# Layer 0 of a four-layer network: x read in 4 KB runs, the group norm's gap filled, pair terms stored by POOL, attention's first rows fed on chip

## The chip, the cores and the metric

The kernel runs on one core of one Trainium2 chip. The metric is the device time of one execution in microseconds (us), as the median of three runs. The engines are PE (matrix products and transposes; PEld is its weight load), DVE (vector), ACT (scalar functions), POOL (general) and SP, which here only issues DMAs. DMAs issued by SP and those issued by POOL run on the same 16 DMA engines of the core. PE writes to PSUM; DVE and ACT read PSUM and SBUF, POOL reads SBUF.

## What is computed

x has 256 x 256 tokens of 128 channels, float32. Four layers follow one another; each takes a group norm of x, computes something from it and adds the result to x. Only layer 0 and the start of layer 1 matter here:

```python
def _L0_conv_ref(x, mask, ln_w, ln_b, w_tri, w_q, w_k, w_v, w_g, b_g, w_o, b_o):
    # H = 4 heads of C = 32; B, I, J, D = 1, 256, 256, 128
    mu = jnp.mean(x, axis=-1, keepdims=True)
    var = jnp.mean(jnp.square(x - mu), axis=-1, keepdims=True)
    xn = (x - mu) * jax.lax.rsqrt(var + EPS) * ln_w + ln_b
    tri_bias = jnp.einsum('bijd,dh->bhij', xn, w_tri)[:, None]
    mask_bias = INF * (mask[:, :, None, None, :] - 1.0)
    q = (xn @ w_q).reshape(B, I, J, H, C) * (1.0 / np.sqrt(C))
    k, v = ...                                   # the same with w_k, w_v
    scores = jnp.einsum('bimhc,binhc->bihmn', q, k) + tri_bias + mask_bias
    attn = jax.nn.softmax(scores, axis=-1)
    o = jnp.einsum('bihmn,binhc->bimhc', attn, v)
    g = jax.nn.sigmoid((xn @ w_g + b_g).reshape(B, I, J, H, C))
    return (g * o).reshape(B, I, J, H * C) @ w_o + b_o

x = x + _L0_conv_ref(_gn(x), ...)    # _gn: mean and variance of 32 groups of 4 channels over all tokens
x = x + _L1_conv_ref(_gn(x), ...)
...
```

The group norm needs all of x before anything else can be computed. The layer norm then needs mean and variance of every token. The tri_bias ("pair term") of one row i of x is needed by every row of attention, so all of x has to be passed over a second time before the first row's softmax.

## The kernel before

`x` lies in memory token by token. The kernel works on its transpose (channels on the 128 partitions), in 32 tiles of SC = 2048 tokens. Tiles 0 to 17 are written transposed to memory (`xT`) in the first pass and read again in the second; tiles 18 to 31 are held in SBUF and written to `xT` during the second pass, because attention reads all of it. CK is 512, P and D are 128, NH is 4, N is 256. Outside of `manual_schedule` the instructions are put into an order by a scheduler; within it, each engine has them in the order of the program.

The first pass, and the folding of weights that follows in the program:

```python
RES = NSC // 2 + 2
with tc.tile_pool(name="x0", bufs=1) as xres, tc.tile_pool(name="p0", bufs=3) as sb:
    held = {s: xres.tile([P, SC], F32, name=f"x0_{s}") for s in range(RES, NSC)}
    with tc.tile_pool(name="p0ps", bufs=6, space=PSUM) as ps:
        for s in range(NSC):
            xt = sb.tile([P, 4, 4, D], F32, name="p0_x", tag="xt")
            nc.sync.dma_start(xt, x_tok[s * SC : (s + 1) * SC, :].rearrange("(c p k) d -> p c k d", p=P, k=4))
            xc = held[s] if s in held else sb.tile([P, SC], F32, name="p0_xc", tag="xs")
            for c in range(4):
                pt = ps.tile([P, P, 4], F32, name="p0_t")
                for k in range(4):
                    nc.tensor.transpose(pt[:, :, k], xt[:, c, k, :], ident)
                pf = pt.rearrange("p n k -> p (n k)")
                nc.vector.bn_stats(stats0[:, s * 4 + c, :], pf)
                nc.scalar.copy(xc[:, c * CK : (c + 1) * CK], pf)
            if s not in held:
                nc.sync.dma_start(xT[:, s * SC : (s + 1) * SC], xc)
    with tc.tile_pool(name="f0", ...) as fsb, tc.tile_pool(name="f0ps", ...) as ps:
        ...   # w0c, cqkg, cv, w2c_, b2w, wsum, kcol, ctri from the weights: small matmuls and copies
```

The second pass: per token the sums that the layer norm needs and the pair terms (`pr`, five rows: four heads and the mean), and the mean of squares (`e2`):

```python
    order = [s for i in range(RES) for s in (RES + i, i) if s < NSC]     # 18, 0, 19, 1, ...
    for _ in range(3):
        fetch(0)                                                          # reads of xT, three ahead
    m0, r0 = gn_finish(stats0, "gn0")                                     # bn_aggr of all entries, then the groups
    ...
    for i, s in enumerate(order):                                         # in manual order
        xc = held[s] if s in held else loaded[s]
        sq = sb.tile([P, SC], F32, name="p1_sq", tag="xt")
        nc.scalar.activation(sq, xc, AF.Square, bias=mrneg, scale=r0)
        pr = ps.tile([P, CK], F32, name="p1_pr")
        ...                                                               # 4 matmuls into pr
        tr = wk_sb.tile([P, CK], F32, name="p1_tr", bufs=3)
        nc.vector.tensor_copy(tr, pr)
        if s in held:
            nc.sync.dma_start(xT[:, s * SC : (s + 1) * SC], xc)
        else:
            fetch(i)
        for c in range(4):
            nc.sync.dma_start(triD[:, s * SC + c * CK : s * SC + (c + 1) * CK], tr[32 * c : 32 * c + 5, :])
        ...                                                               # 4 matmuls of the sq before into e2
    for c in range(4):
        nc.sync.dma_start(mean[32 * c : 32 * c + 32, :], by_c[c])         # the means back, from triD
    ...                                                                   # mean, square, e2 - square, max, Sqrt
    nc.vector.reciprocal(mean, var)
    for c in range(4):
        nc.sync.dma_start(rs_c[c], mean[32 * c : 32 * c + 32, :])         # 1/std to memory (rsD)
```

The setup of attention, up to its loop:

```python
    nc.sync.dma_start(tri..., triD...)                                    # pair terms, a pool of its own ("p2i")
    nc.sync.dma_start(mk, mbD...)
    nc.sync.dma_start(rs, rsD...)                                         # 1/std back from memory
    for h in range(NH):
        ... (tri + toff) * rs                                             # DVE
    ...                                                                   # 20 transposes, + ctri on DVE: triT, mbT
    load(0)        # x of group 0 (4 rows) from xT, 1/std of it from rsD, broadcast to all partitions
    prepare(0)     # ACT: x - mean; POOL: times 1/std
    tiles(0)
    for c in range(2):
        for what in "qkvg":
            project(0, what, c)
    load(1)
    prepare(1)
    for j in range(2 * NG + 5):
        ...        # the loop over pairs of rows
```

Layer 1 begins with a folding of its own. Its tile `cen` lies in a pool ("f1") whose room the first loads of layer 1 take over:

```python
    with tc.tile_pool(name="f1", bufs=1) as sb, tc.tile_pool(name="f1ps", ...) as ps:
        ...                                         # v1, v2, vb1, vb2, wgf, bgf: need the group norm
        nc.tensor.matmul(pb, lhsT=wz0, rhs=ln2b, ...)
        cen = sb.tile([P, 4, 32], F32, name="f1_c")
        ...                                         # memset, 8 affine_select on POOL
        nc.vector.tensor_scalar(wz4, wz4, g4, None, ALU.mult)
        nc.tensor.matmul(pw, lhsT=cen..., rhs=wz4, ...)
        nc.vector.tensor_copy(wzc, pw)
```

Of the kernel before, what the change touches and what calls it, by code (L numbers as in the profile page):

```python
# [8 lines left out]
F32 = mybir.dt.float32  # L9
# [22 lines left out]
def kernel(ctx: ExitStack, tc: tile.TileContext, a: dict, out: bass.AP):  # L32
# [127 lines left out]

    def gn_finish(stats, name):

        mv = const.tile([P, 2], F32, name=name + "_mv")
        nc.vector.bn_aggr(mv, stats.rearrange("p n s -> p (n s)"))
        return gn_groups(mv, name)
# [38 lines left out]
    w0c = const.tile([P, 4 * D + NH], F32, name="w0c")  # L204
    slide = const.tile([P, 63], F32, name="slide")
# [3 lines left out]
    with tc.tile_pool(name="x0", bufs=1) as xres, tc.tile_pool(name="p0", bufs=3) as sb:  # L209
        held = {s: xres.tile([P, SC], F32, name=f"x0_{s}") for s in range(RES, NSC)}  # L210
        with tc.tile_pool(name="p0ps", bufs=6, space=PSUM) as ps:
            for s in range(NSC):
                xt = sb.tile([P, 4, 4, D], F32, name="p0_x", tag="xt")
                nc.sync.dma_start(
                    xt, x_tok[s * SC : (s + 1) * SC, :].rearrange("(c p k) d -> p c k d", p=P, k=4)
                )
                xc = held[s] if s in held else sb.tile([P, SC], F32, name="p0_xc", tag="xs")
                for c in range(4):
                    pt = ps.tile([P, P, 4], F32, name="p0_t")
                    for k in range(4):  # L220
                        nc.tensor.transpose(pt[:, :, k], xt[:, c, k, :], ident)
                    pf = pt.rearrange("p n k -> p (n k)")
                    nc.vector.bn_stats(stats0[:, s * 4 + c, :], pf)
                    nc.scalar.copy(xc[:, c * CK : (c + 1) * CK], pf)
                if s not in held:
                    nc.sync.dma_start(xT[:, s * SC : (s + 1) * SC], xc)

        with tc.tile_pool(name="f0", bufs=1) as fsb, tc.tile_pool(name="f0ps", bufs=1, space=PSUM) as ps:
            cen = fsb.tile([P, P], F32, name="f0_c")
            nc.vector.tensor_scalar(cen, ident, -1.0 / D, None, ALU.add)  # L230
            wa = fsb.tile([P, 4 * D + NH], F32, name="f0_a")
            nc.vector.tensor_scalar(wa, w0, ln_w, None, ALU.mult)
            wb = fsb.tile([P, 4 * D + NH], F32, name="f0_b")
            nc.vector.tensor_scalar(wb, w0, ln_b, None, ALU.mult)
            for lo, hi in ((0, 4 * D), (4 * D, 4 * D + NH)):
                pc = ps.tile([P, hi - lo], F32, name="f0_pc", tag=f"f0_pc{lo}")
                nc.tensor.matmul(pc, lhsT=cen, rhs=wa[:, lo:hi], start=True, stop=True)
                nc.vector.tensor_copy(w0c[:, lo:hi], pc)
# [1415 lines left out]
```

## Time and profile before

| | before |
|---|---|
| median of 3 runs | 3493.64 us (3487.25 to 3499.86) |
| span of the profiled execution | 3506.8 us |
| PE, DVE, ACT, POOL busy | 89%, 66%, 56%, 46% of the span |
| DMA | 759.49 MB, mean 217 GB/s |

The page cuts the span into 40 slices of 87.7 us and gives for each engine the busy share in tenths. PE is at 3, 6, 7, 5 in the first four slices and at 9 from the fifth on to the seventeenth, which is attention. A busy share over the whole span says nothing about any one stage; for that the trace is asked for stretches of time. A line of instructions reads: start, duration, engine, line of the program, operation, output and inputs, and in brackets how long the engine stood idle before it and what released it. A line of waits reads: engine and line that waited, what it waited for, the sum in us, how many times, the longest. "SPq" is SP issuing DMAs; an instruction of the DMA kind is listed at its issue, not at its landing.

### The profile page before, as it was taken

How to read it: one execution, taken by the hardware profiler on the slowest of the kernel's cores; microseconds unless marked ns; L12 is line 12 of the kernel's file. 1: busy time of each engine (PE TensorE's matmuls, PEld its weight loads, DVE VectorE, ACT ScalarE, POOL GpSimd, SP SyncE). 2: the span in 40 equal slices, each digit the busy share in tenths (PEclk: the TensorE clock that was granted, in tenths of full speed). 3: DMA queues.
4: the chain of work that ended last, by engine and by line, in shares of the span. 5: the costliest groups of instructions: out<-in, count | busy, mean ns of one | idle time of the engine just before them, and what ended most of it. 6: DMA issues, size and time to landing. Idle time of an engine off the chain costs nothing.

```text
span 3506.8 us, 52443 instructions
## 1 busy us (share of the span) xinstructions
PE 3133.7 (89%) x20260; PEld 1652.1 (47%) x20260; DVE 2321.5 (66%) x2637; ACT 1961.4 (56%) x2198; POOL 1605.4 (46%) x821
## 2 busy tenths in 40 slices
PE   3675999999999999966597899999999999959998
PEld 3512555555555555521432344444899533314444
DVE  4624888888888888852388454544555677747776
ACT  3563777777777777733243454443444466636655
POOL 4002777777777777732488000000555354514343
PEclk7887999999999999978799899999999999969999
DMA  9883333333333333349599686775999899747664
GB/s 334 324 317 113 98 123 114 106 122 115 105 122 111 109 122 112 108 156 387 173 321 356 228 312 244 284 270 193 342 353 351 307 335 322 277 168 204 193 200 133
DMA packets 309867, 759.49 MB, mean 217 GB/s; under 512 B 77627, under 2 KB 148957, under 8 KB 259437
## 3 DMA queue, kind: packets, MB, share of 16 engines
q1 hardware_dynamic: 298749, 746.43, 60.9%
q0 software_dynamic: 10864, 9.65, 0.9%
q8 instruction: 162, 2.65, 0.3%
q14 instruction: 92, 0.75, 0.1%
HBM read 468.28 MB, written 287.66 MB: 216 GB/s over the span
## 4 chain that ended last, share of the span: by engine, by line
PE 38%; DMA 7%; DVE 2%; ACT 1%; SPq 1%; issue 1%; POOL 0%; ACTq 0%; DVEq 0%; POOLq 0%
PE p_pm L946 13%; PE tp_z L1612 6%; PE p_pm L1099 4%; PE p_pm L1334 4%; PE p_pg L810 3%; DMA x3T<-p_x 2%; PE tp_a L1601 2%; PE p_st L903 1%; PE p_pt L1371 1%; PE p_pz L818 1%; DMA p_er<-eD 1%; DMA x2T<-p_x 1%; DMA p_x<-x3T 1%; PE p_eb L860 1%; PE p_rz L860 1%
## 5 line engine op out<-in xcount | busy, mean ns | idle before, releaser
L489 DVE TENSOR_TENSOR p_e<-p_S,triT 128x1024 f32<-128x1024 f32 x512 | 609.0, 1211 | 144.7 <-PE p_S L479 144.7
L499 POOL TENSOR_TENSOR p_es<-p_e 128x1024 f32<-128x1024 f32 x256 | 603.1, 2367 | 127.4 <-issue 67.3
L497 ACT ACTIVATE p_e<-p_e,mbT 128x1024 f32<-128x1024 f32 x512 | 551.8, 1137 | 63.0 <-DVE p_e L489 61.2
L946 PE MATMUL p_pm<-p_zn,wf 128*128 128x512 f32 x1040 | 450.0, 594 | 1.4 <-DVE p_zn L963 1.4
L464 PE MATMUL p_mm<-p_xn,wf 128*128 128x512 f32 x768 | 409.2, 617 | 9.2 <-POOL p_xn L437 9.2
L437 POOL TENSOR_TENSOR p_xn<-p_xn,p_rs 128x1024 f32<-128x1024 f32 x64 | 153.5, 2398 | 452.2 <-DMA p_rs<-rsD 259.9
L946 PEld LDWEIGHTS p_pm<-p_zn,wf 128*128 128x128 f32 x1040 | 197.6, 191 | 254.6 <-issue 247.8
L479 PE MATMUL p_S<-p_q,p_k 32*128 32x256 f32 x4096 | 295.4, 400 | 5.0 <-DVE p_e L489 5.0
L479 PEld LDWEIGHTS p_S<-p_q,p_k 32*128 32x128 f32 x4096 | 185.8, 184 | 161.5 <-PE p_mm L455 91.7
L1348 POOL TENSOR_TENSOR p_q<-p_q,p_pb 128x2024 f32<-128x2024 f32 x32 | 144.1, 4503 | 254.8 <-DVE p_pb L1342 254.8
L1612 PE MATMUL tp_z<-p_B,tp_at 128*128 128x256 f32 x1024 | 250.2, 387 | 2.4 <-DMA p_B<-bD 2.2
L512 PE MATMUL p_o<-p_e,p_v 128*32 128x256 f32 x4096 | 249.2, 384 | 0.0
L1012 POOL DMA_DIRECT2D rs__18024<-rs2D x4 | 2.1, 520 | 531.7 <-PE p_pm L946 531.7
L1055 POOL TENSOR_TENSOR k<-k,p_sq 128x512 f32<-128x512 f32 x128 | 163.1, 1274 | 135.2 <-ACT p_sq L1053 135.2
L1165 POOL TENSOR_TENSOR p_x<-p_x,p_g 128x2048 f32<-128x2048 f32 x30 | 136.2, 4542 | 171.9 <-DVE p_g L1152 137.8
L1612 PEld LDWEIGHTS tp_z<-p_B,tp_at 128*128 128x128 f32 x1024 | 185.1, 191 | 24.5 <-issue 2.5
L464 PEld LDWEIGHTS p_mm<-p_xn,wf 128*128 128x128 f32 x768 | 126.8, 191 | 114.6 <-issue 90.3
L1054 DVE TENSOR_TENSOR k<-tp_z,k 128x512 f32<-128x512 f32 x128 | 88.6, 692 | 128.4 <-ACT p_sq L1053 128.4
L512 PEld LDWEIGHTS p_o<-p_e,p_v 128*32 128x32 f32 x4096 | 120.4, 110 | 110.1 <-ACT p_g L470 41.5
L979 DVE SCALAR_TENSOR_TENSOR p_b<-p_pm,b2w,p_b 128x1024 f32<-128x1024 f32 x64 | 82.2, 1284 | 126.6 <-PE p_pm L946 112.2
L455 PEld LDWEIGHTS p_mm<-wf,p_xn 128*128 128x128 f32 x1024 | 135.3, 192 | 62.8 <-issue 61.9
L1051 ACT COPY p_K<-tp_z 128x512 f32<-128x512 f32 x128 | 74.9, 585 | 159.7 <-PE tp_z L1612 159.7
(353 smaller groups left out, 5903.8 us busy)
## 6 DMA issues: line engine op xcount, KB each, us to landing
p_x<-x2T SPq DMA_DIRECT2D x64, 1024.0 KB
p_x<-x1T SPq DMA_DIRECT2D x48, 1024.0 KB
p_x<-in_x_dram SPq DMA_DIRECT2D x32, 1024.0 KB
p_x<-xT SPq DMA_DIRECT2D x64, 512.0 KB
p_rs<-rsD SPq DMA_DIRECT2D x64, 512.0 KB
p_rb<-rzD SPq DMA_DIRECT2D x256, 128.0 KB
x1T<-p_x SPq DMA_DIRECT2D x64, 512.0 KB
aD<-p_a SPq DMA_DIRECT2D x32, 1024.0 KB
```

Of the source, the lines that this page charges most:

```text
L437: nc.gpsimd.tensor_tensor(xn, xn, t["rs"], ALU.mult)
L464: nc.tensor.matmul(pm, lhsT=w, rhs=t["xn"][:, cs_], start=True, stop=True)
L479: nc.tensor.matmul(Ss[h // 2][:, h % 2, u, :], lhsT=t["k"][hp, r * N + u * P : r * N + (u + 1) * P], rhs=t["q"][hp, r * N : (r + 1) * N], ...
L489: nc.vector.tensor_tensor(e[:, :, 2 * p : 2 * p + 2, :].rearrange("p u h n -> p h u n"), Ss[p], triT[:, 2 * p : 2 * p + 2, :, :], ALU.add,)
L497: nc.scalar.activation(e[:, u, :, :], e[:, u, :, :], AF.Exp, bias=mbT[:, u, i : i + 1])
L499: nc.gpsimd.tensor_tensor(es, e[:, 0, :, :], e[:, 1, :, :], ALU.add)
L512: nc.tensor.matmul(t["o"][hp, r % 2, :], lhsT=t["v"][:, r * 2 + u, hp], rhs=e[:, u, h, :], start=(u == 0), stop=(u == 1),)
L946: nc.tensor.matmul(pm[:, c, :], lhsT=wf2[:, i, :], rhs=zns[s][:, k * CK : (k + 1) * CK], start=True, stop=True)
L1055: nc.gpsimd.tensor_tensor(k2, k2, sq, ALU.add)
L1099: nc.tensor.matmul(pm[:, c, :], lhsT=w, rhs=src[:, k * CK : (k + 1) * CK], start=True, stop=True)
L1348: nc.gpsimd.tensor_tensor(q[:, :, 1 : N - 2], q[:, :, 1 : N - 2], pb[:, :, 0 : N - 3], ALU.add)
L1612: nc.tensor.matmul(pz[:, t, :], lhsT=at[:, u, t * P : (t + 1) * P], rhs=Bc[:, u, :], start=(u == 0), stop=(u == 1))
```

## The change

It touches only what lies before attention's loop and the beginning of layer 1. What it does, and what for:

- **First pass.** A partition takes 8 tokens in a row (4 KB) instead of 4 (2 KB), so that a load has half as many pieces. The eight transposes of a block lie side by side in a PSUM tile[...]; the interleaving of tokens is done by ACT, which reads that tile with a stride. The pass is in manual order: the load of three tiles ahead is issued right after a tile's transposes, before its store.
- **Folding.** The folding of all weights, layer 1's `bz` and `wzc` included, is done after tile 12 of the first pass.
- **Group norm.** All statistics but the last four entries are aggregated one tile early and merged with the rest afterwards; meanwhile the first five held tiles are stored to `xT`.
- **Second pass.** POOL issues the stores of the pair terms.
- **Setup.** 1/std stays on chip (`rs0`): a matmul with a selector broadcasts it for the first 1024 tokens, and transposes turn it for the pair terms, which are loaded and turned while it is still being computed. Only the first half of group 0 is projected before the loop.

```diff
+            def load0(s):
+                if s < NSC:
+                    xts[s] = sb.tile([P, 2, 8, D], F32, name="p0_x", tag="xt")
+                    nc.sync.dma_start(
+                        xts[s], x_tok[s * SC : (s + 1) * SC, :].rearrange("(c p k) d -> p c k d", p=P, k=8)
+                    )
+            def folds():
+                ...   # the folding of layers 0 to 3, two PSUM buffers
+            for s in range(3):
+                load0(s)
             for s in range(NSC):
...
-                for c in range(4):
-                    pt = ps.tile([P, P, 4], F32, name="p0_t")
-                    for k in range(4):
-                        nc.tensor.transpose(pt[:, :, k], xt[:, c, k, :], ident)
...
+                for c in range(2):
+                    pt = ps.tile([P, 8, P], F32, name="p0_t")
+                    for k in range(8):
+                        nc.tensor.transpose(pt[:, k, :], xt[:, c, k, :], ident)
+                    for h in range(2):
+                        nc.vector.bn_stats(stats0[:, s * 4 + 2 * c + h, :], ...)
+                    nc.scalar.copy(
+                        xc[:, c * 2 * CK : (c + 1) * 2 * CK].rearrange("p (n k) -> p n k", k=8),
+                        pt.rearrange("p k n -> p n k"),
+                    )
+                load0(s + 3)
                 if s not in held:
                     nc.sync.dma_start(xT[:, s * SC : (s + 1) * SC], xc)
+                if s == 12:
+                    folds()
+                if s == NSC - 2:
+                    mv_first = gn_part(stats0, 0, T // CK - 4, "gn0_a")
...
-        m0, r0 = gn_finish(stats0, "gn0")
+        early = range(RES, RES + 5)
+        for s in early:
+            nc.sync.dma_start(xT[:, s * SC : (s + 1) * SC], held[s])
+        mv0 = gn_merge(mv_first, gn_part(stats0, T // CK - 4, T // CK, "gn0_b"), 1.0 - 4.0 * CK / T, "gn0_mv")
+        m0, r0 = gn_groups(mv0, "gn0")
...
-                    if s in held:
+                    if s not in held:
+                        fetch(i)
+                    elif s not in early:
                         nc.sync.dma_start(xT[:, s * SC : (s + 1) * SC], xc)
-                    else:
-                        fetch(i)
                     for c in range(4):
-                        nc.sync.dma_start(
+                        nc.gpsimd.dma_start(
                             triD[:, s * SC + c * CK : s * SC + (c + 1) * CK], tr[32 * c : 32 * c + 5, :]
                         )
...
+                nc.scalar.activation(mean, mean, AF.Square, bias=off[:, 4:5])
...
+                nc.vector.reciprocal(rs0, var)
...
+            load_x(0)
+            tri = ...                                   # load of the pair terms, of the mask, of x for group 1
+            for c in range(4):
+                nc.sync.dma_start(rs_c[c], rs0[32 * c : 32 * c + 32, :])
+            load_rs(1)
+            xn = centre(0)
+            ...                                         # 20 transposes; ACT copies, + toff: triT, mbT
+            rb = [...]                                  # two matmuls: rs0 broadcast for tokens 0 to 1023
+            ...                                         # four transposes: rsT
             tiles(0)
             for c in range(2):
-                for what in "qkvg":
-                    project(0, what, c)
-            load(1)
+                nc.vector.tensor_tensor(xn[:, c * CK : (c + 1) * CK], xn[...], rb[c], ALU.mult)
+                for h in (2 * c, 2 * c + 1):
+                    nc.vector.tensor_tensor(triT[:, h, :, :], triT[:, h, :, :], rsT, ALU.mult)
+            project(0, "q", 0)
+            project(0, "k", 0)
+            for h in range(NH):
+                nc.scalar.activation(triT[:, h, :, :], triT[:, h, :, :], AF.Identity, bias=ctri[:, h : h + 1])
+            project(0, "v", 0)
+            project(0, "g", 0)
             prepare(1)
             for j in range(2 * NG + 5):
...
+                if j == 0:
+                    for what in "qkvg":
+                        project(0, what, 1)
...
-    with tc.tile_pool(name="f1", bufs=1) as sb, tc.tile_pool(name="f1ps", bufs=1, space=PSUM) as ps:
+    with tc.tile_pool(name="f1ps", bufs=1, space=PSUM) as ps:
...                                                      # bz, cen, wz4, wzc gone from here
```

## Prediction

> **What bounds the kernel now.** I read the page's slices first (which engine is full when), then the table of busy time by stretches cut at the borders of the change, then the waits of the DMA-issuing engine SP, and last the timeline around each border. The stretches are: first pass over x, group norm, second pass over x, setup of attention, attention, start of layer 1, its first pass.
>
> ```profile
> 0.00:164.00 164.00, 78.49 (x512) 73.36 (x512) 84.37 (x147) 74.62 (x128) 35.27 (x73) 0.77 0.94 338
> 164.00:182.00 18.00, 14.83 (x74) 8.23 (x78) 10.55 (x31) 8.52 (x8) 0.00 (x0) 0.72 0.37 143
> 182.00:278.00 96.00, 64.80 (x486) 17.07 (x478) 21.23 (x38) 58.98 (x29) 0.00 (x0) 0.86 0.87 323
> 278.00:318.00 40.00, 13.44 (x48) 8.48 (x48) 12.96 (x16) 6.51 (x8) 2.34 (x1) 0.62 0.38 119
> 318.00:1537.00 1219.00, 1206.07 (x12260) 668.38 (x12259) 1020.43 (x1083) 865.14 (x954) 900.47 (x383) 0.99 0.34 110
> 1537.00:1563.00 26.00, 5.98 (x35) 3.84 (x37) 12.91 (x23) 1.54 (x2) 1.40 (x8) 0.57 0.45 165
> ```
>
> The last two figures of a row are the DMA share and GB/s; before them come PE, PEld, DVE, ACT, POOL and the clock. Both passes over x are DMA-bound (0.94 and 0.87). The group norm (18 us) and the setup (40 us) are bound by nothing that is full: they are chains. Attention is bound by PE, 1206 of 1219 us, and the change leaves its loop alone. So all it can earn lies in the 318 us ahead of attention and in the 26 us behind it.
>
> The waits of SP, first pass, then second pass:
>
> ```profile
> SPq L226 <- ACT p_xc L224: 49.0, 18, 6.8
> SPq L214 <- PE p_t L221: 38.6, 15, 3.8
> ```
> ```profile
> SPq L336 <- DMA p_xc<-xT: 25.0, 15, 3.2
> SPq L336 <- DMA xT<-x: 11.5, 13, 1.2
> ```
>
> In the first pass SP stands before stores that wait for copies while free buffers could be loaded. In the second, the small pair stores (L336) wait for large transfers to land: by the order of the issues, SP can go on only when the DMA issued eight before has landed (POOL shows the same count in the weights: its ninth waited 2.11 us for its first), and eight of every ten DMAs here are 10 KB stores. So hardly more than one load and one store are in flight.
>
> The timeline at the borders:
>
> ```profile
> 37.55 0.38 DVE L694 TENSOR_SCALAR wz<-wz,g 128x128 f32<-128x128 f32 x1 [16.39 <-DMA g<-in_L_conv_ln_g_dram]
> ...
> 164.11 3.62 DVE L164 BATCH_NORM_AGGREGATE gn_mv<-stats 128x2 f32<-128x768 f32 x1
> ...
> 175.34 2.10 ACT L321 ACTIVATE p_sq<-x,mrneg,gn_rstd 128x2048 f32<-128x2048 f32 x1 [0.47 <-DVE mrneg L294]
> ...
> 281.32 0.48 DVE L353 TENSOR_SCALAR p_mean<-p_mean,p_off 128x512 f32<-128x512 f32 x1 [4.86 <-DMA p_mean<-triD]
> ...
> 284.58 3.35 DVE L358 RECIPROCAL p_mean<-p_var 128x512 f32<-128x512 f32 x1 [0.79 <-ACT p_var L357]
> ...
> 293.88 2.74 DVE L391 SCALAR_TENSOR_TENSOR tri<-tri,toff,p_rs 128x512 f32<-128x512 f32 x4 [5.96 <-DMA p_rs<-rsD]
> ...
> 307.19 2.34 POOL L437 TENSOR_TENSOR p_xn<-p_xn,p_rs 128x1024 f32<-128x1024 f32 x1 [259.89 <-DMA p_rs<-rsD]
> ...
> 319.57 2.35 DVE L489 TENSOR_TENSOR p_e<-p_S,triT 128x1024 f32<-128x1024 f32 x2 [1.24 <-PE p_S L479]
> ```
> ```profile
> 1557.47 0.29 DVE L697 COPY wzc<-f_w 128x128 f32<-128x128 f32 x1 [0.89 <-PE f_w L696]
> 1557.51 0.33 SPq L707 DMA_DIRECT2D x<-x1T  x1
> ...
> 1562.87 3.29 PE L712 MATMUL p<-x,v 128*32 128x512 f32 x16 [5.44 <-DMA x<-x1T]
> ```
>
> Layer 1's weight folding, pulled ahead by the scheduler, holds DVE 16.4 us in the first pass. Statistics end at 164.1 and the second pass starts 11.2 us later. In the setup 1/std goes to memory and back twice (to 293.88 for the pair terms, to 307.19 for x). At 1557.5 the first load of layer 1 waits until the folding lets go of its buffer.
>
> **What the Trainium skill says.** "Perfetto Trace Analysis", section "DMA Optimizations", holds that 2 KB pieces made into 4 or 8 KB can improve throughput dramatically. The trace does not promise that: 54.37 MB in 91.4% of the first 164 us is 363 GB/s of busy queue with mostly 2 KB pieces; the second pass, mostly 8 KB, moves 30.90 MB in 86.7% of 96 us, 371 GB/s. "DMA: Bandwidth & Descriptors", section "Issuing engines are not separate DMA queues", says that another issuing engine saves only issue time; here it should also give SP its places in flight back. The same page, section "Anatomy of one DMA — SWDGE (gpsimd) path", gives some 2 us fixed per DMA issued by POOL; this trace has 5.2 to 5.4 us to landing for tiny weight loads beside full queues. "ScalarE: Activation LUTs", section "What ACT_TABLE_LOAD costs", gives about 280 ns + 0.833 ns per element: 1.13 us for 1024, and the trace has 1.137 for Exp of that size, 1.016 for a plain copy out of PSUM. It says nothing of a strided read of PSUM, which the new copy does.
>
> **The change part by part.**
>
> *First pass.* 32 loads and 18 stores of 1.049 MB are 52.4 MB. Now they end near 160 and the last statistics at 164.1, 4 us of lag. At 367 GB/s, midway between the two rates because runs of x double, they take 143 us; the weights (2.5% of 164) add 4, the start 2. Laying transposes side by side saves nothing on PE: 273 ns median here, 273 in layer 3's contiguous ones. The folding, now in order after tile 12, costs about 13 us of DVE and PE: 8 us that its matmuls spanned at 164.8, 2 of scalings then done early, 3.2 of the group-mean matrix at 1554.6. Of this the queue (two loads and a store, some 8 us) hides most; 3 to 5 us stay. The 10 us of DMA idle (6% of 164) shrink to little else. Sum: 143 + 4 + 2 + 4 (folding) + 4 (lag) = 157, less some 2 us that runs of 4 KB may save beyond the midway rate: last statistics at **155**, gain **9**.
>
> *Group norm.* Of the 3.62 us aggregation all but four entries lie earlier; five small DVE steps of 0.16 to 0.22 come in. The part from there to the first Square took 2.5 us (172.84 to 175.34). So 4.3 us instead of 11.2. The 7 us do not count by themselves, since the second pass is DMA-bound: what counts is that the queue stays full. Five stores, 5.2 MB or 14 us, behind three prefetches do that.
>
> *Second pass.* From the last landing of x, 155 - 4 = 151: 18 loads and 14 stores, 33.55 MB at 371 GB/s, are 90 us, pair terms and mask (1.8 MB) 5. At a busy share of 0.97 that is 98; plus 3 us from landing to the last pair copy gives 252, where it was 276.5. ACT needs 32 x 2.09 = 67 us, so it isn't the bound. Gain at this point **24**, the first pass included.
>
> *Setup.* Before: last pair copy at 276.5, first bias add 319.6: 43 us. After: four POOL stores 2.2 us (0.53 each in the weights), landing 2.5, mean loads 1.7 + 1.7, then Square to reciprocal 6.4 as now: 1/std at +14.5 (now +11.5, as SP's stores cost less). The raw pair terms arrive and are turned by about +16, beside it. Then broadcast and turning of 1/std on PE 3, first half of x and two pair planes on DVE 2, q and k 3.5 with a cold clock, v and g 3, scores 1: the first add at about +28. That is 15 us less; the second half of group 0's projections (4.1 us by 1.02 each) moves into the first rows, where PE has little room. Net **11**.
>
> *Start of layer 1.* Without the folding's buffer, its first load can go out at about 1548 with the two others. DMA stands idle from about 1554 to 1558 now and the pass after it is DMA-bound (0.95). Gain **5**.
>
> Sum: 24 + 11 + 5 = 40; 3493.6 - 40 = **3453 us**.
>
> **The rivals.**
>
> *POOL's pair stores become the bound of the second pass.* Eight in flight with 5.3 us to landing is 0.66 us per store, 2.65 per tile, against 2.8 of DMA per megabyte at 371 GB/s: nearly equal. With 6.5 us to landing it is 3.25 per tile, 104 us from 160: the second pass ends at 264 and the gain falls to 28 (3466). For it: 51.4 us of DVE waiting for these stores already. Against it: POOL has nothing else to do then.
>
> *The strided copy out of PSUM is slow.* If 1024 elements cost 2.2 us instead of about 1.1, ACT needs 4.4 per tile; the 14 tiles that are only loaded, at 2.8 now, lose 22 us: 3475. No row here shows such a read, for or against.
>
> *The queue fills perfectly.* No stall of the folding, 376 GB/s throughout, POOL free: 148 for the first pass, 243 for the second, and the setup earns 15: gain 54, 3440. For it: shares of 0.98 in the tail of the first pass (120 to 150 us).
>
> *Attention gives it back.* Its start could be pushed by the second half of the projections and the wait for group 1's 1/std through memory; 5 us at most, since both were on the path before.
>
> **Range and chances.** The first two rivals bound it above, the third below; with a few us of spread between runs (3487 to 3500 before) I take 3436 to 3472. A gain of over 2%, 70 us, would need more than all idle DMA time of the two passes and the whole setup; a loss of 70 has no mechanism. Faster 0.03, same 0.95, slower 0.02.
>
> **What would show it.** Last statistics near 155, first Square within 5 us of it with the DMA share over 0.9 through the gap; last pair copy near 252, SP no longer waiting for landings at the pair stores, POOL perhaps doing so; first bias add some 28 us after the last pair copy; the first load of layer 1 issued with its neighbours. Wrong would be: a copy much over 1.2 us per 1024 elements, DVE waiting over 50 us for the pair stores, or a DMA share in the passes no better than before.

## The result, and the profile after

The changed kernel takes 3471.67 us (median of 4 runs, 3464.3 to 3479.48), the kernel before in the same comparison 3491.65. The ratio is 0.994 with a 95% interval of 0.9911 to 0.997: some 20 us gained, where 40 were predicted (3453) and up to 3472 allowed for. Both kernels were compared once more on another occasion, with a ratio of 0.9908 (0.9883 to 0.9934) and medians 28 us apart. Runs of one kernel spread over 15 us and more, so below the stages are compared by the trace and only the sums by the medians.

Stretches of the changed kernel, cut at the same events as before the change (columns: stretch in us, its length, busy us of PE, PEld, DVE, ACT and POOL, granted clock, DMA share, GB/s):

```profile
0.00:162.00 162.00, 97.38 (x550) 83.53 (x550) 92.43 (x175) 64.79 (x64) 36.71 (x81) 0.75 0.89 350
162.00:167.00 5.00, 1.17 (x4) 1.00 (x4) 1.85 (x12) 2.66 (x4) 0.00 (x0) 0.50 1.00 423
167.00:264.00 97.00, 65.80 (x514) 16.22 (x514) 23.66 (x41) 66.52 (x33) 59.91 (x121) 0.92 0.84 315
264.00:295.00 31.00, 11.06 (x58) 7.61 (x58) 8.93 (x10) 8.15 (x13) 3.53 (x8) 0.63 0.33 113
295.00:1516.00 1221.00, 1207.43 (x12262) 668.91 (x12258) 1024.04 (x1088) 868.15 (x959) 900.57 (x383) 0.99 0.33 110
1516.00:1537.00 21.00, 3.02 (x28) 2.58 (x32) 9.22 (x15) 1.54 (x2) 0.00 (x0) 0.50 0.56 201
```

The group norm shrank from a gap of 11 us with a mostly idle queue to 5 us with a full one. Attention is as long as before. But the DMA share, which was to rise, is *lower* in the first pass (0.89, was 0.94) and in the second (0.84, was 0.87). The first pass is cut finer here:

```profile
40.00:68.00 28.00, 17.39 (x93) 15.83 (x94) 13.22 (x21) 10.12 (x10) 8.22 (x15) 0.63 1.02 413
68.00:98.00 30.00, 18.21 (x76) 14.43 (x73) 12.23 (x38) 3.60 (x4) 1.57 (x8) 0.60 0.43 174
98.00:160.00 62.00, 41.55 (x274) 35.43 (x272) 45.59 (x69) 34.88 (x35) 0.00 (x0) 0.83 1.01 398
```

A full queue at about 400 GB/s on both sides (a share of 1 or a little above is a full queue), and a hole of 30 us at less than half of that. In the hole lies the weight folding. The waits of SP, first pass and then second pass, and those of DVE and POOL in the second:

```profile
SPq L240 <- PE p_t L331: 81.0, 24, 24.3
SPq L343 <- ACT p_xc L337: 33.9, 18, 2.5
```
```profile
SPq L357 <- PE p_pr L421: 57.6, 12, 7.1
SPq L403 <- DVE mk L402: 11.8, 1, 11.8
```
```profile
DVE p_tr L427 <- DMA triD<-p_tr: 52.4, 22, 6.0
...
POOL triD L433 <- DMA triD<-p_tr: 22.0, 23, 1.8
```

One load of x (L240) stood 24.3 us before tiles that PE had not transposed. In the second pass SP no longer waits for landings, as predicted. It waits for a buffer of x that PE is still to read; PE waits for DVE; DVE waits 52.4 us for the pair stores of three tiles before; and POOL, which issues them, waits for its own landings. The timeline at the borders:

```profile
74.05 0.23 DVE L255 TENSOR_SCALAR f_s<-ident 128x128 f32<-128x128 f32 x1 [3.83 <-issue]
...
92.85 0.29 DVE L321 COPY wzc<-f_w 128x128 f32<-128x128 f32 x1 [0.95 <-PE f_w L320]
...
96.01 1.01 ACT L337 COPY p_xc<-p_t 128x1024 f32<-128x1024 f32 x1 [24.69 <-PE p_t L331]
...
162.23 0.26 DVE L164 BATCH_NORM_AGGREGATE gn_b<-stats 128x2 f32<-128x24 f32 x1
...
167.28 2.09 ACT L418 ACTIVATE p_sq<-x,mrneg,gn_rstd 128x2048 f32<-128x2048 f32 x1 [0.42 <-DVE mrneg L372]
...
263.28 0.69 DVE L427 COPY p_tr<-p_pr 128x512 f32<-128x512 f32 x1 [1.57 <-DMA triD<-p_tr]
...
273.52 3.35 DVE L453 RECIPROCAL rs<-p_var 128x512 f32<-128x512 f32 x1 [0.79 <-ACT p_var L452]
276.95 0.39 SPq L633 DMA_DIRECT2D tri<-triD  x1
...
295.24 2.36 DVE L550 TENSOR_TENSOR p_e<-p_S,triT 128x1024 f32<-128x1024 f32 x2 [1.45 <-PE p_S L540]
...
1515.79 3.62 DVE L745 BATCH_NORM_AGGREGATE chk_mv<-stats 128x2 f32<-128x768 f32 x1
...
1525.35 3.62 DVE L181 BATCH_NORM_AGGREGATE gn_mv<-stats 128x2 f32<-128x768 f32 x1 [4.70 <-DVEq L754]
...
1531.37 0.17 DVE L200 RECIPROCAL gn_rstd<-gn_sd 128x1 f32<-128x1 f32 x1 [0.99 <-ACT gn_sd L198]
1531.56 0.33 SPq L791 DMA_DIRECT2D x<-x1T  x1
...
1536.60 3.33 PE L796 MATMUL p<-x,v 128*32 128x512 f32 x16 [3.73 <-issue]
```

The lines of before that belong beside these, where the prediction does not show them:

```profile
275.77 0.69 DVE L330 COPY p_tr<-p_pr 128x512 f32<-128x512 f32 x1 [2.64 <-DMA triD<-p_tr]
...
1540.50 3.62 DVE L638 BATCH_NORM_AGGREGATE chk_mv<-stats 128x2 f32<-128x768 f32 x1
...
1547.06 3.62 DVE L164 BATCH_NORM_AGGREGATE gn_mv<-stats 128x2 f32<-128x768 f32 x1 [1.64 <-SPq L647]
```

Against before: last pair copy done at 263.97 (was 276.46, 12.5 earlier); from there to attention's first bias add 31.3 us (was 43.1, 11.8 less); attention to its last aggregation at 1515.79 1220.6 us (was 1220.9); from there to the first matmul of layer 1 20.8 us (was 22.4). Together 26 us. The last of these hides two parts. Between attention's last aggregation and the group norm's (the two lines with chk_mv and gn_mv) lies a branch of the program, behind which DVE stood idle 4.70 us (was 1.64). From the group norm's aggregation to the matmul it took 11.3 us (was 15.8), 4.6 less. Four holes are left to explain: the folding (68 to 98), the second pass that is not full, the load of the pair terms (276.95) that goes out only after the reciprocal, and layer 1's first load (1531.56), which does the same.

### The profile page after: what moved, and what is told of

Its sections match the earlier page's. It is cut to its first block, busy times and chain, and to the rows that moved or that the text cites. A ratio compares the mean times of both kernels' runs of the same rounds, so it can differ in the third digit from the quotient of the medians.

```text
span 3477.7 us, 52488 instructions
## 1 busy us (share of the span) xinstructions
PE 3130.0 (90%) x20268; PEld 1652.2 (48%) x20268; DVE 2319.3 (67%) x2639; ACT 1957.9 (56%) x2144; POOL 1666.4 (48%) x948
## 4 chain that ended last, share of the span: by engine, by line
PE 38%; DMA 11%; DVE 2%; SPq 2%; issue 2%; ACT 1%; POOL 1%; ACTq 0%; DVEq 0%; POOLq 0%
PE p_pm L1030 13%; PE tp_z L1696 7%; PE p_pm L1183 6%; DMA p_x<-x3T 3%; DMA x2T<-p_x 2%; PE p_pm L1418 2%; DMA abD<-p_ab 2%; PE tp_a L1685 2%; PE p_pg L894 2%; PE p_st L987 2%; DMA p_t<-tD 1%; PE p_rz L944 1%; PE p_rk L944 1%; SPq L1305 1%; PE p_pz L902 1%
## 5 line engine op out<-in xcount | busy, mean ns | idle before, releaser
L516 PEld LDWEIGHTS p_mm<-wf,p_xn 128*128 128x128 f32 x1024 | 134.4, 191 | 61.9 <-issue 59.8
## 6 DMA issues: line engine op xcount, KB each, us to landing
p_rb<-rzD SPq DMA_DIRECT2D x256, 128.0 KB
```

## The experiments

Each is an edit of the changed kernel. First that kernel itself, as a control.

> The changed kernel again, nothing edited: 3472 us within 8. Last statistics near 162, first Square near 167, last pair copy near 264, first bias add near 295. It stands here so that the edits of it are read against it on the same chip.

Measured: 3470.82 us (3462.75 to 3482.41); last statistics at 160.71, first Square at 165.77, last pair copy done at 263.26, first bias add at 296.00. What follows is compared with 3471. The runs were made on four occasions, on which the kernel before had medians from 3495 to 3512 us. So a few us between medians of different occasions show little by themselves, and the stages are read from the traces.

**The folding in pieces.** The folding becomes a generator with 14 `yield` lines, two of them in loops of two, so it runs in 17 pieces; after every half tile from tile 9 on one piece is issued. Its scratch gets a pool of its own, as it now lives longer.

```diff
-                scratch = sb.tile([P, SC], F32, name="f0_s", tag="xs")
+                scratch = fsb.tile([P, SC], F32, name="f0_s")
...
+                yield                      # after each step of folds() that the next one waits for
...
+                    if s >= 9:
+                        next(fold, None)
                 load0(s + 3)
...
-                if s == 12:
-                    folds()
```

> The folding of the weights is cut into 15 pieces, one after each half tile from tile 9 on, with scratch room of its own; nothing else differs from the changed kernel. Theory: done in one piece after tile 12 it stopped PE and DVE for some 19 us and emptied the DMA queue (share 0.43 from 68 to 98 us), so cut up the last statistics come at 147 instead of 162 and the time falls by 15 us, to 3457. Rival: the folding costs its own work wherever it stands, because DVE and PE have little room in the first pass: no more than 5 us.

Measured: 3452.26 us (3448.52 to 3455.08), 18.6 less than the control. The same stretch in its trace, and the last statistics:

```profile
68.00:98.00 30.00, 20.98 (x128) 18.80 (x126) 17.57 (x38) 12.15 (x12) 1.57 (x8) 0.77 1.02 424
```
```profile
143.37 0.26 DVE L164 BATCH_NORM_AGGREGATE gn_b<-stats 128x2 f32<-128x24 f32 x1
```

The queue is full throughout (1.02 for 0.43), the last statistics come at 143.37 instead of 160.71, and the 17 us reach the end. The folding is a chain in which DVE and PE wait for each other: 18.8 us from 74.05 to 92.85 in the changed kernel. Engines in strict order did nothing for x meanwhile. SP issued nothing between 71.35 and 96.04, and what was in flight kept the queue full only to about 80 us; from 82 to 95 it moved 4 GB/s. In pieces the same chain has other work between its steps. One thing is not kept apart: before the chain DVE stood 3.83 us. The scratch takes one of the three buffers of the stores in the changed kernel, and this edit also gives it room of its own. Whether that was the wait, and so up to 3.8 of the 18.6 us, is not shown.

**The mask ahead.** The mask's load, its conversion and its store to memory move from the start of the second pass to tiles 4 and 6 of the first.

```diff
-            mk = wk_sb.tile([P, 2, N], F32, name="mk", bufs=1)
-            nc.sync.dma_start(mk, a["L0_conv_mask"]...)      # and its conversion, and the store to mbD
...
+                if s == 4:
+                    mk = msb.tile([P, 2, N], F32, name="mk")
+                    nc.sync.dma_start(mk, a["L0_conv_mask"]...)
+                if s == 6:
+                    ...                                      # conversion, store to mbD
```

> The mask is loaded, converted and stored during tiles 4 to 6 of the first pass instead of at the start of the second; nothing else differs from the changed kernel. Theory: in the second pass the mask's load lies behind eight megabytes that now fill the gap, SP stands 11.8 us before the mask's store and cannot issue reads of x, and the DMA share falls to 0.36 between 176 and 184 us; with the mask gone from there the share stays over 0.9 and the time falls by 8 us, to 3464. Rival: POOL's pair stores bound the second pass at about 3 us per tile anyway, so it falls by 2 us at most.

Measured: 3475.31 us (3466.32 to 3485.54), no gain. SP's wait at the mask is gone, yet from first Square to last pair copy it takes 102.1 us where the control takes 97.5. DVE waits for the pair stores for 61.9 us (52.4 in the changed kernel):

```profile
DVE p_tr L428 <- DMA triD<-p_tr: 61.9, 20, 8.4
```

The mask was not what ended this pass. That the pair stores were is shown by the run with half as many stores below.

**Pair stores by SP again.** One word: the stores of `p1_tr` are issued by `nc.sync` instead of `nc.gpsimd`.

> The pair stores are issued by SP again; nothing else differs from the changed kernel. Theory that POOL's stores (5.5 us to landing, eight in flight) bound the second pass: it gets shorter by about 5 us, DVE's 52 us of waiting for these stores falls below 25, and the mean is back sooner after the last pair copy. Rival, the purpose of the change: SP's places in flight are what matters, and the second pass gets longer by 5 to 10 us, with SP waiting for landings of x at the pair stores (25 us in the kernel before).

Measured: 3472.94 us, ratio to before 0.9932 (0.9911 to 0.9954) against the control's 0.9908 (0.9883 to 0.9934). Six of its 20 executions, and eight of the 20 of the run on layer 1's first load below, lie apart at 3510 to 3524 us, and without them the medians are 3471.4 and 3473.1. Neither expectation shows in the time, and this part of the change is not seen to earn anything: in the changed kernel SP's waits for landings went, and the same kind of wait came up at POOL. That agrees with the Trainium skill, "DMA: Bandwidth & Descriptors", section "Issuing engines are not separate DMA queues", by which another issuing engine saves only the time of issuing, and not with the places in flight that I added to it.

**Runs of 2 KB again.**

```diff
-                    xts[s] = sb.tile([P, 2, 8, D], F32, name="p0_x", tag="xt")
+                    xts[s] = sb.tile([P, 4, 4, D], F32, name="p0_x", tag="xt")
...              # the load with k=4, and the transposes and the copy that fit it
```

> The changed kernel with one thing put back: x is loaded in runs of 2 KB again (each partition takes four consecutive tokens in each of four blocks, not eight in each of two); transposes side by side, the one copy of 1024 per half tile and all else stay. Theory (longer runs move more per busy us): outside the folding's window the first pass falls from 387-394 GB/s to about 360 at the same DMA share near 1, so its 52 MB take some 9 to 11 us longer and the whole kernel 8 to 11 us: about 3481. Rival (the gain came from loads issued ahead of the stores, and the run length is indifferent): DMA rate within 5 GB/s of the changed kernel's, time within 3 us of 3471. A rate that falls while the time stays would say that something else ends the first pass.

Measured: 3475.59 us (3472.68 to 3478.46), 4 to 5 more, on another occasion than the control.

```profile
40.00:68.00 28.00, 15.72 (x90) 14.42 (x89) 13.14 (x21) 10.10 (x11) 9.03 (x16) 0.76 1.04 408
98.00:160.00 62.00, 38.47 (x267) 33.53 (x265) 43.39 (x66) 33.84 (x34) 0.00 (x0) 0.86 1.02 377
```

The first of these stretches before the change:

```profile
40.00:68.00 28.00, 13.34 (x86) 12.89 (x84) 15.18 (x27) 13.32 (x24) 6.45 (x11) 0.70 0.89 308
```

408 for 413, 377 for 398. Seven traces with the unchanged first pass have between 373 and 398 in the second stretch, 387 in the mean, so the run length is worth some 10 GB/s there if anything, under 2 us of the 62. The last statistics come at 162.93, inside what those traces spread over (159.1 to 164.9). The large gain that the Trainium skill, "Perfetto Trace Analysis", section "DMA Optimizations", holds possible is not there, and the rise from 308 GB/s between 40 and 68 us (before) to 413 has another cause.

**The store ahead of the load.** The remaining difference in the queue's order: SP issues the store of tile s before the load of tile s + 3, as before the change.

```diff
-                load0(s + 3)
                 if s not in held:
                     nc.sync.dma_start(xT[:, s * SC : (s + 1) * SC], xc)
+                load0(s + 3)
```

> The changed kernel with two lines of the first pass in the other order: in each tile SP issues the store of tile s first and the load of tile s + 3 after it, as in the kernel before; runs of 4 KB, side-by-side transposes and all else stay. Open since the run with 2 KB runs: why the first pass moves 408-413 GB/s between 40 and 68 us (before: 308), if the run length is worth 1% of it. Theory (SP stands before a store that waits for the copies of its tile while a free buffer could be loaded, so fewer transfers are in flight): the rate between 40 and 68 us falls to 370 or less at a DMA share below 0.97, the last statistics come 5 to 10 us later (166 to 171) and the time is 3476 to 3482. Rival (three loads ahead and the short copies are enough in either order; what held the kernel before was the scheduler's placement of the weight folding and of the copies): rate over 400, last statistics within 2 us of 161 to 162, time within 4 us of 3471.

Measured: 3473.78 us (3465.88 to 3476.85); 407 GB/s from 40 to 68 us, 371 from 98 to 160; last statistics at 165.02. The rate from 40 to 68 us and the time, within 4 us, are the rival's; the last statistics lie 3 us later than it allows, and 0.1 outside what the seven traces spread over. Neither run length nor this order makes the 413 by itself. What is left is the fixed order as a whole (before, a scheduler placed the pass, and DVE stood 16.4 us in it, though that ended at 37.55) and the two put back together; neither was tried, and the cause stays open.

**No stores in the gap.** `early = range(0)`: the five stores that fill the group norm's gap go out in the second pass instead.

> The changed kernel without the five stores of x that fill the gap of the group norm: they are made in the second pass instead, each behind its tile's copies. Theory A (the second pass is bound by the bytes of its queue, as I predicted): 5.2 MB more at some 370 GB/s, 14 us, come onto the path, the last pair copy comes 12 to 14 us later after the first Square (110 instead of 97 us) and the time is about 3484. Theory B (the second pass is bound by the return of the pair stores to their three buffers): the second pass has 17% of idle queue to take them in, so its length grows by 0 to 5 us, its DMA share rises from 0.83 to 0.9 or more, and the time is within 5 us of 3471.

Measured: 3471.36 us (3462.72 to 3474.83), as the control. The second pass, from first Square to last pair copy, of this run and then of the changed kernel:

```profile
164.14:266.97 102.83, 66.00 (x514) 15.27 (x514) 23.40 (x39) 67.16 (x33) 60.08 (x121) 0.95 0.87 319
```
```profile
167.28:263.97 96.69, 65.80 (x514) 16.22 (x514) 23.42 (x39) 66.52 (x33) 59.88 (x121) 0.92 0.84 315
```

5.2 MB more lengthen the pass by 5 to 6 us, not by 14. The share rises to 0.87 only, where theory B had 0.9 or more, but the pass had idle queue to take most of the bytes. From first Square to first bias add (298.79) it takes 134.7 us, 130.2 in the control and 128.0 in the changed kernel. So while something else ended the pass, the filled gap earned 4 to 7 us in this stage, of which the median shows nothing.

**1/std in place.** `p1_mean` and `p1_var` are dropped and their steps are worked out in `rs0`, which lives on:

```diff
-                    nc.sync.dma_start(mean[32 * c : 32 * c + 32, :], by_c[c])
-                var = wk_sb.tile([P, CK], F32, name="p1_var", bufs=1)
+                    nc.sync.dma_start(rs0[32 * c : 32 * c + 32, :], by_c[c])
...
-                nc.vector.reciprocal(rs0, var)
+                nc.vector.reciprocal(rs0, rs0)
```

> The changed kernel with mean and variance of the setup worked out in place in the tile that lives on (rs0), so that no tile of the second pass's pool is read after its last pair store and the load of the raw pair terms need not wait for the reciprocal. Theory (the first bias add is held by that load, which went out at 276.95 behind the reciprocal at 273.5 although the data were there from about 266): the load goes out right behind the four mean loads, about 268 to 270, the first bias add comes 5 to 8 us earlier (24 to 26 us after the last pair copy instead of 31), time about 3465. Rival (the projections or the 1/std chain hold the first add and the raw terms only arrive beside them): first bias add at most 1 us earlier, 3470 to 3472.

Measured: 3464.52 us (3458.4 to 3469.09), 6 to 7 less.

```profile
272.12 0.72 ACT L447 ACTIVATE rs<-rs,p_off 128x512 f32<-128x512 f32 x1 [10.08 <-DMA rs<-triD]
272.87 0.39 SPq L631 DMA_DIRECT2D tri<-triD  x1
...
274.81 3.35 DVE L451 RECIPROCAL rs<-rs 128x512 f32<-128x512 f32 x1 [0.79 <-ACT rs L450]
...
285.30 1.28 DVE L671 TENSOR_TENSOR triT<-triT,p2i_rs 128x512 f32<-128x512 f32 x2
```

The load of the pair terms goes out before the reciprocal. The first product of triT with 1/std comes 20.1 us after the last pair copy (265.16), in the changed kernel 25.4 (289.40 after 263.97); the first bias add (291.47) comes 26.3 after it instead of 31.3. The load had waited for memory of the second pass's pool, not for the reciprocal's result. Read the same way, it still waits: the edit was meant to leave no tile of that pool that is read so late, but the Square of the means reads one more (`p1_off`). The load starts 0.03 us after that Square ends, 2.4 us after the loads of the means were issued, and just so in the run with half as many stores and in the one with everything. So up to 2.4 us may be left here; no run frees this tile.

**Five buffers for the pair terms**, on top of that: `bufs=3` becomes `bufs=5`.

> As the run with the in-place 1/std, and the pair terms have five buffers between VectorE's copy and their stores instead of three. To be compared with that run. Theory B (the return of the pair stores holds the second pass: VectorE waits 52 us for it in the changed kernel, with a median of 5.5 us to landing): those waits fall below 25 us, the DMA share of the second pass rises to 0.9 or more and the last pair copy comes 6 to 10 us earlier after the first Square (about 88 instead of 97): about 3457. Rival A (the mask's load and store in order before the fetches, and the bytes of the queue): the waits move to ScalarE for fetched x, the pass gets at most 3 us shorter: 3462 to 3465. Rival C (POOL's eight DMAs in flight hold it, whatever the buffers): POOL waits for landings rise from 22 us by what VectorE loses, the pass stays at 97.

Measured: 3460.56 us (3453.92 to 3467.59) against 3464.52, not to be told apart. The pass is 91.0 us instead of 95.2, but what follows, to the first product of triT, grows from 20.1 to 24.8. DVE waits 48.7 us for the stores (57.9 with three buffers), POOL 16.9 for landings (19.8): neither theory B's fall below 25 nor rival C's rise. Why, its timeline and its pair stores (duration of one, first and last start) show:

```profile
253.47 11.81 POOL L433 DMA_DIRECT2D triD<-p_tr  x24 [0.36 <-DVE p_tr L427]
...
257.26 0.69 DVE L427 COPY p_tr<-p_pr 128x512 f32<-128x512 f32 x1 [1.45 <-DMA triD<-p_tr]
...
265.03 1.83 SPq L446 DMA_DIRECT2D rs<-triD  x4
```
```profile
L433 POOL DMA_DIRECT2D triD<-p_tr x128: 497/497/542, 172.8 to 264.8; - x128
```

When the last pair copy is done (257.95), POOL still has some 15 of these 24 stores to issue, and the loads of the means wait for the last. Buffers only move the queue of stores. From the first to the last, POOL needs 92.0 us for 128, 0.72 us each: 0.50 of issuing, the rest waiting, mostly for landings. That this rate is the bound is what the next run tests.

**Half as many stores.** On top of 1/std in place, two tiles share one buffer, and one store takes both. The mask, converted at the start of the pass, borrows one of these buffers (left out below).

```diff
-                    tr = wk_sb.tile([P, CK], F32, name="p1_tr", bufs=3)
-                    nc.vector.tensor_copy(tr, pr)
+                    if i % 2 == 0:
+                        lo, hi = sorted(order[i : i + 2])
+                        tr = wk_sb.tile([P, 2, CK], F32, name="p1_tr", bufs=3)
+                    nc.vector.tensor_copy(tr[:, int(s == hi), :], pr)
...
-                    for c in range(4):
+                    for c in range(4) if i % 2 else ():
                         nc.gpsimd.dma_start(
-                            triD[:, s * SC + c * CK : s * SC + (c + 1) * CK], tr[32 * c : 32 * c + 5, :]
+                            triD.rearrange("h (s c t) -> h s c t", c=4, t=CK)[:, lo : hi + 1 : hi - lo, c, :],
+                            tr[32 * c : 32 * c + 5, :, :],
                         )
```

> As the run with the in-place 1/std (3464.5), but the pair terms of two tiles are kept in one buffer (three buffers of 4 KB a partition) and go out in one store per partition group: 64 stores of 20 KB instead of 128 of 10 KB, same bytes, still by POOL. Theory (POOL's rate of stores is the bound of the second pass: with five buffers POOL still needed 92 us for 128, 0.72 each, and had a backlog of 24 stores, 11.8 us, when the last data had landed): 64 stores take some 45 to 50 us of issuing and waiting, POOL keeps up, the second pass becomes bound by the queue: 84 to 89 us from first Square to last pair copy (95 there), DMA share 0.92 or more, the first bias add stays 20 us behind, time 3454 to 3458. Rival (the bytes or the landing of the stores count, not their number): VectorE still waits over 40 us for landings, the pass stays at 91 to 95, time 3460 to 3465.

Measured: 3453.92 us (3451.49 to 3455.97), 10.6 less than with 1/std in place alone; from first Square to first bias add it takes 110.8 us, 121.5 there.

```profile
166.57:250.29 83.72, 64.37 (x510) 18.23 (x514) 23.30 (x39) 65.27 (x33) 33.70 (x60) 0.92 0.93 363
```
```profile
DVE p_tr L429 <- DMA triD<-p_tr: 9.6, 3, 5.0
...
POOL triD L435 <- DMA triD<-p_tr: 2.3, 1, 2.3
```

The pass is 83.7 us long, the DMA share 0.93. DVE's wait for the stores fell from 57.9 to 9.6 us, POOL's from 19.8 to 2.3. The bytes are the same and the median landing is no shorter (5.9 us). Three buffers of two tiles are also more room than three of one, but five of one had left the pass and what follows it, to the first product, at 115.8 us (115.3 with three); here they take 104.2. So the number of stores was the bound. Whether through the time of issuing or through the landings that POOL waits for is not kept apart.

**Layer 1's first load.** In the group norm's helper the scratch columns `d` and `sd` are allocated in `const` instead of in a pool whose room layer 1's x takes over.

> The changed kernel with one thing at the start of layer 1: the two one-column scratch tiles of the group means (d and sd) are allocated among the constants instead of in a pool that is freed before layer 1's x tiles are placed. Theory (the first load of x1 was issued only at 1531.56, behind the reciprocal that last reads that pool, 8 us after the two loads next to it at 1523): it goes out with its neighbours about 1523, the first matmul of the pass comes 2 to 4 us earlier after the aggregation (17 to 19 us instead of 20.8), and the time is 2 to 4 us less, about 3468. Rival (the first matmul waits for v, which needs the same reciprocal, and then for whatever the queue brings): the load moves, the first matmul at most 1 us; time unchanged within the spread. Not to be told apart by the time alone, as runs of one kernel differ by 10 us: the trace decides.

Measured: 3479.16 us (3465.17 to 3522.23, 20 runs), ratio 0.9947 (0.9918 to 0.9976): a gain of 2 to 4 us cannot be read from times that spread so far. The trace shows it:

```profile
1527.76 3.62 DVE L745 BATCH_NORM_AGGREGATE chk_mv<-stats 128x2 f32<-128x768 f32 x1
...
1537.67 0.35 SPq L791 DMA_DIRECT2D x<-x1T  x1
...
1543.15 0.16 DVE L200 RECIPROCAL gn_rstd<-gn_sd 128x1 f32<-128x1 f32 x1 [0.97 <-ACT gn_sd L198]
...
1544.89 3.64 PE L796 MATMUL p<-x,v 128*32 128x512 f32 x16 [0.25 <-DVE bgf L782]
```

The load goes out 5.5 us before the reciprocal instead of 0.2 after it, and the first matmul comes 17.1 us after the aggregation instead of 20.8. It is now released by the last of the folded weights and no longer stands behind the load. That is 3.7 us.

**All of them.** Folding in pieces, mask ahead, 1/std in place, two tiles per store, scratch in `const`.

> All that the runs point to in one kernel: weight folding cut into 15 pieces spread over the tiles from the ninth on, mask loaded and stored in the first pass, pair terms of two tiles in one store, 1/std in place, the scratch of the group means among the constants. If the parts add: folding 18.6, in-place 1/std 6.5, half the stores 6 to 10, layer 1 start 2 to 4, and the mask, which earned nothing while the pair stores were the bound, 3 to 6: 3471 less 36 to 45 = about 3431, ratio to before 0.98. If they do not (each brings the second pass only to the same floor): folding and 1/std alone, 3471 - 25 = 3446.

Measured: 3432.56 us (3421.3 to 3437.35, 6 runs), ratio to the kernel before 0.9798 (0.9769 to 0.9826). It beats both kernels, the changed one by 38 us, so the parts add as expected (36 to 45). Its second pass:

```profile
149.62:230.53 80.91, 63.76 (x510) 18.01 (x514) 23.07 (x38) 65.15 (x33) 33.70 (x60) 0.93 0.95 368
```

From first Square to first bias add (255.08) it takes 105.5 us; 110.8 without folding and mask moved (277.39 after 166.57), 128.0 in the changed kernel. The folding in pieces alone does not shorten this stage (127.7). So the mask ahead, worth nothing alone, seems to be worth some 5 us once the stores no longer end the pass. Part of it may be the buffer that the mask borrowed in the run it is compared with: DVE waits 2.9 us for it there.

## Why the prediction was 19 us off and still in its range

*First pass (155, gain 9).* Measured 162.2 and 160.7, gain 2 to 3. The step that failed is the folding's: "some 13 us of DVE and PE", of which the queue was to hide some 8, leaving 3 to 5. What was in flight did last some 9 us, but nothing was issued for 24.7 us: 3.8 of waiting, 18.8 of the chain and 2.9 from its end to the next load. Cutting it up gave 18.6 us. The rate was mis-sized the other way: 367 GB/s was put down, 398 to 413 measured around the hole, and the reason given, longer runs, is worth some 10 GB/s at most. The two errors nearly cancel, so the 155 is close by luck: with the folding in pieces the pass ends at 143, 12 us earlier than predicted. The strided copy takes 1.01 us per 1024 elements, so that rival was wrong. PE had nothing from side-by-side transposes to show, as said (a median of 273 ns before and after).

*Group norm (first Square within 4.3 us, queue full).* 5.05 us and a share of 1.00: right, 0.8 over.

*Second pass (bound by the queue at a share of 0.97, last pair copy 252).* 264, at a share of 0.84. The step that failed is the choice of the bound. The first rival, POOL's pair stores, is what happened. That it also had the end at 264 is luck: it counted 104 us from 160, and measured are 96.7 from 167.3. Its arithmetic was one DMA in eight landing in turn; measured are 0.50 us of issue and waits, mostly for landings, to a sum of 0.72 to 0.73 per store. The sentence that spoke against it, that POOL has nothing else to do, was true and beside the point. Two of the three signs that the prediction gave for being wrong came: DVE waits 52.4 us for these stores, over the 50 (but 51.4 before the change), and the DMA share of the two passes is no better than before.

*Setup (first bias add at +28, 15 less, net 11).* +31.3, 11.8 less. The net is right by chance: the raw pair terms were to arrive and be turned by +16 beside the 1/std chain, but their load went out at +13 (276.95), held by buffer reuse, and they were turned only from 283.16, at +19. On the other side the 4 us that I let attention lose for the second half of the projections did not show: 1220.6 us against 1220.9. The same attention takes 1218.7 to 1224.0 us in the traces of the edits, so a loss of a few us could hide in one pair; the last rival is not seen, but not excluded either.

*Start of layer 1 (gain 5).* 1.6. The part that the prediction spoke of came near its size: from the group norm's aggregation to the first matmul 4.6 us less, without the folding of before. What it did not have is the branch ahead of it, 3.1 us longer (4.70 for 1.64); why stays open (below). And its reason failed: the first load did not go out with its neighbours (1523) but at 1531.56. The folding's buffer did go away; a second one behind it, one column of the group norm's scratch, held the same load. Freed, it gives 3.7 more.

Sum on the chip by these stages: 12.5 + 11.8 + 0.3 + 1.6 = 26 for 24 + 11 + 5 = 40. The range held by less than 2 us (3471.67 and 3470.82 for an upper end of 3472), and only because it was drawn for rivals of which the first came true, not for the path that the prediction held likely.

## What to carry to other kernels

A small chain of dependent steps dropped in one piece into a streaming loop can cost its whole length, less what is still in flight, when every engine keeps program order: cut it and lay a piece beside each tile. Ask of many small DMAs how many there are and what one costs its issuer, rather than who issues them or how many buffers they have; here another issuer moved the wait, more buffers moved it to the end, and fewer and larger stores removed it. When a transfer starts right behind an instruction whose result it doesn't use, look for the pool whose memory it takes over, and for its very last reader: freeing one tile may only uncover the next.

## What was not expected of the hardware

A store of two tiles' pair terms costs POOL 0.56 us to issue, one of half the size 0.50. Landing takes some 5.5 us either way beside full queues (medians 5.5 and 5.9).

The program's branch after attention lets DVE start again after 4.45 to 4.88 us in the traces of the changed kernel and of most edits, but after 1.34 in those with half as many stores and with everything (1.64 before the change). So it is part of what the changed kernel gained too little at layer 1, and of what those two runs gained. No edit aimed at it, and what sets it stays open. The layer's start with everything, 14.5 us, has 3.3 us of its gain from there.

Traces whose first pass is the same instruction for instruction move between 373 and 398 GB/s from 98 to 160 us; differences of that size between two single traces mean nothing.
